# A four-layer network with a scheduled main loop: the TensorE part of the loop traced in program order

## The chip, the cores and the metric

The kernel runs on one core of a Trainium2 chip. The metric is the device time of one execution in microseconds (us). Engines are named as in the profile: PE (TensorE matmul), PEld (its weight loads), DVE (VectorE), ACT (ScalarE), POOL (GpSimd) and SP (SyncE, which issues most DMAs).

## The reference

Input x is fp32, 8 samples of 512 channels and 32 by 32 pixels, that is 512 x 1024 per sample. Four layers follow each other:

```
# layer 0: attention without softmax, scaled by the largest singular value
z = f_x^T g_x ; z2 = (z / sigma_max(z)) h_x ; x = Wv z2 + x
# layer 1: group norm, then full attention over the 1024 pixels
q,k,v = wq h, wk h, wv h ; x = x + wp softmax(q^T k / sqrt(512)) v
# layer 2: non-local block with 128 channels
t,p,g = split(W_w x) ; x = bn(Z_w softmax(t^T p / sqrt(128)) g) + x
# layer 3: binarised 1x1 convolution, batch norm, residual, shifted PReLU
x = prelu(bn(sign(W) scale . sign(x + b)) + x)
```

All 8 samples pass layers 1 to 3 one by one; only the batch norms of layer 0 need all samples at once.

## The kernel before

The kernel is one Python function that records instructions for a scheduling layer. That layer receives the instructions in program order, orders those of each engine by its own estimate of when they can run, and sets all semaphores. Inside `with tc.manual_schedule(engines={PE})` it keeps the recorded order on PE; the other engines are still ordered by it. The kernel already does so for the last part of layer 0 (from L1585), but not for the main loop.

**Main loop.** `for n in range(B): hb, ua = fast(env, n, hb, ua)` (L1661) takes one sample through layers 1 to 3. `fast` (L919) records, in this order: `scores1` (layer 1's score matrix), `make_v`, `values1`, `project2` (layer 2's projections), `scores2`, `values2` and `close2` (layer 2's output), and `leave` (layer 3). PE work of the neighbouring samples is woven in by Python generators: `make_u` of the next sample runs between the steps of layer 2, and the second half of `leave` of the sample before is held in the list `rest3` and run between the first steps of the next sample's `scores1`.

**The seven-product scheme.** The large fp32 matrix products are made as 2 x 2 blocks with seven block products instead of eight (`seven`, L350; the operands' sums are made on DVE in `sums_of` and `differences_of`). A block product is a `term`: two fp32 matmul instructions of 128x512 at L413. Several terms accumulate into one PSUM bank, and partial sums are read out between them, for example

```
term(pa, "S3", "T3", False, False)
plus(va, b2, c22, c22)            # DVE reads the bank (L366)
...
term(pa, "A22", "T4", False, True)
move(c21, va, b2)                 # ACT reads it (L360)
then()                            # in make_u: the sums of ut, L331 to L336
```

The second term may only write the bank when the read before it is done. In `make_u` the last term of the second group is the pair of matmuls shown as `bank<-hs,wu`; the reads of the partial sums are the DVE instructions L366 (`ut<-bank,bu,ut`). In `scores1` the first term is the pair `bank<-ut,h`, its read is the ACT copy L358 (`e<-bank`); the next terms are `us,hs` (S1 T1), `us,hs` (S2 T2, into the first bank), `us,h` (S4 B22) and `ut,h` (S3 T3, into the first bank again, after another L358 copy of it).

**Layer 3.** `leave` (L713) makes sign(x) in fp16 on ACT (L720, `sg`), then for each of two output pairs j four fp16 matmuls (L732, `bank<-sg,sw`), after which come ACT L743, DVE L744, L745, L753 (twice), ACT L775 and L776 (twice each) and DVE L783 (twice), and a DMA to the output. For the last sample the matmuls use `signs`, and L759 (DVE), L762 (ACT), L769 (POOL) take part.

**The boundary between two samples.** There are seven of them. PE's program order there is: the last terms of `make_u` (`h,wu`, `h,wu`, `hs,wu`), then the first score term of the next sample (`ut,h` twice), then four L732 matmuls of the sample before.

**The end.** For the last sample, `inverse_rows` (L887) sums the softmax denominators on PE (L892, from `esum`, which DVE L852 makes) and takes reciprocals on DVE (L893). `count_bad` (L801) checks the denominators' range: a one-column matmul L823, a DVE cast to an integer `bad` (L824), and `values_load` (L825), which every engine runs as a register load (TENSOR_LOAD) of `bad` for the branch `tc.If(verdict[0] > 0)` (L1777). The branch is not taken with these inputs.

Of the kernel before, what the change touches and what calls it, by code (L numbers as in the profile page):

```python
# [17 lines left out]
B = 8  # L18
# [69 lines left out]
def kernel(  # L88
# [39 lines left out]
    def psum_pools(stack, wides, banks):  # L128
        psum.clear()
        for name, n in (("wide", wides), ("bank", banks)):  # L130
            if n:
                psum[name] = stack.enter_context(
                    tc.tile_pool(name=f"{name}{n}", bufs=n, space=PSUM, reuse_waits="tile")
                )
# [342 lines left out]
    def normal(env, xt, alone=False):  # L477

        sc, bi = norm
        ht = env["big"].tile([P, CC, N], F32, tag="h", name="h")  # L480
        for ns in [half(h) for h in range(NH)] if alone else [slice(0, N)]:
            for cc in range(CC):
                s1, b1 = sc[:, cc : cc + 1], bi[:, cc : cc + 1]
                hs, xs = ht[:, cc, ns], xt[:, cc, ns]
                if cc % 2 and not alone:
                    nc.scalar.activation(hs, xs, AF.Identity, bias=b1, scale=s1)
                else:
                    nc.vector.tensor_scalar(hs, xs, s1, b1, ALU.mult, ALU.add)  # L488
        return ht
# [3 lines left out]
    def split_h(env, ht):  # L493
        hs = env["big"].tile([P, 3, 2, HF], F32, tag="hs", name="hs")
        b = [ht[:, chunks[k], half(n)] for k in range(2) for n in range(2)]
        return differences_of(b, [hs[:, i] for i in range(3)])

    def make_u(env, hb, got, early=False):

        ut = env["big"].tile([P, CC, N], F32, tag="uv", name="ut")  # L500
        wa = weights["u"]

        def done():
            us = env["big"].tile([P, 3, 2, HF], F32, tag="us", name="us")
            got.append(
                sums_of(quarters_of(ut, chunks, [half(0), half(1)]), [us[:, i] for i in range(3)])
            )

        def group(i):
            term = product_of(  # L510
                lambda a, b, q, k: wa[a][:, k, bass.ts(i, P)],
                lambda a, b, q, k: hb[b][:, k, :],
            )
            return seven(
                term,
                ut[:, i, half(0)],
                ut[:, i, half(1)],
                ut[:, 2 + i, half(0)],
                ut[:, 2 + i, half(1)],
                bu[:, i : i + 1],  # L520
                bu[:, 2 + i : 3 + i],
                then=done if i else None,
                early=early,
            )

        groups = [group(i) for i in range(2)]
        for _ in range(2 * early):
            for g in groups:
                next(g)
                yield  # L530
        for g in groups:
            yield from g
# [729 lines left out]
    env = {}  # L1262
# [386 lines left out]
    with ExitStack() as main:  # L1649
        psum_pools(main, 0, 8)  # L1650
        big = main.enter_context(tc.tile_pool(name="big", bufs=1, reuse_waits="tile"))
        epool = main.enter_context(tc.tile_pool(name="epool", bufs=EBUFS))
        small = main.enter_context(tc.tile_pool(name="small", bufs=3))
        env.update({"big": big, "e": epool, "small": small})
        got = []
        hb = split_h(env, normal(env, resident[order[0]], True))

        for _ in make_u(env, hb, got, True):
            pass
        ua = got[0]  # L1660
        for n in range(B):  # L1661
            hb, ua = fast(env, n, hb, ua)


    def attention(env, scores, scale, apply):
# [111 lines left out]
    with tc.If(verdict[0] > 0):  # L1777
        with (
# [5 lines left out]
            env = {"big": big, "e": epool, "small": small}  # L1784
# [49 lines left out]
```

## Time and profile before

| | |
|---|---|
| median of 3 runs | 1872.2 us (1871.53 to 1872.94) |
| time of the profiled execution | 1872.37 us |
| its span, first to last instruction | 1870.5 us |
| PE busy, 6196 matmul records | 1850.9 us |
| DVE busy | 1121.5 us |
| ACT busy | 541.7 us |
| granted TensorE clock | 0.998 |

The span is 1.9 us shorter than the execution's time. An fp32 matmul instruction of 128x512 shows as two records that start 0.43 us apart, so it takes 0.86 us of PE's time; the record's own duration (0.59 us) overlaps the next. An fp16 one of the same shape is one record, 0.22 us from the next. Lines are numbered as in the kernel before; in the changed kernel all lines after L1660 are one higher.

### The profile page before, as it was taken

To read this page: it belongs to the slowest core of one execution; us is meant where nothing else is said; L and a number is where in the kernel's file an instruction comes from. 1 tells how busy PE (TensorE), PEld (TensorE's weight loads), DVE (VectorE), ACT (ScalarE), POOL (GpSimd) and SP (SyncE) were. 2 spreads that over 40 slices of the span, in tenths; PEclk is the share of its full clock that TensorE was granted. 3 is DMA by queue.
4 is the path that set the end of the run, shared out by engine and by line. 5 is a ranking of instruction groups with operands and counts; after the bars stand their busy time and mean duration, and the time that the engine had idled before them with its cause. 6 is when DMAs were issued, how large, how long until landed. Compare 5 with 4: busy or idle time off the path is not lost.

```text
span 1870.5 us, 16535 instructions
## 1 busy us (share of the span) xinstructions
PE 1850.9 (99%) x6196; PEld 948.9 (51%) x6196; DVE 1121.5 (60%) x2083; ACT 541.7 (29%) x882; POOL 121.8 (7%) x109
## 2 busy tenths in 40 slices
PE   9999999999999999999999999999999999999997
PEld 4365464544644464544645455544644464544653
DVE  3356777467745767567754676357643766355447
ACT  2042221243213521244202521244203521244114
POOL 1000002000010001100020001100010001000011
PEclk9999999999999999999999999999999999999999
DMA  8620000002000200012000200001000200000001
GB/s 282 201 86 7 1 18 1 1 34 73 12 1 12 90 17 1 0 35 73 12 1 12 90 18 0 1 34 68 12 0 12 90 12 0 1 34 23 12 0 47
DMA packets 32738, 66.52 MB, mean 36 GB/s; under 512 B 4944, under 2 KB 12300, under 8 KB 32524
## 3 DMA queue, kind: packets, MB, share of 16 engines
q1 hardware_dynamic: 31724, 64.96, 10.2%
q8 instruction: 51, 0.84, 0.2%
q10 hardware_dynamic: 864, 0.43, 0.1%
q14 instruction: 35, 0.29, 0.0%
q0 software_dynamic: 64, 0.00, 0.0%
HBM read 46.44 MB, written 18.94 MB: 35 GB/s over the span
## 4 chain that ended last, share of the span: by engine, by line
PE 96%; DVE 2%; ACT 1%; issue 0%; DMA 0%; POOL 0%; ACTq 0%; DVEq 0%
PE bank L413 46%; PE bank L591 21%; PE bank L993 6%; PE bank L840 6%; PE bank L1382 4%; PE bank L692 3%; PE bank L709 3%; PE bank L732 1%; PE bank L437 1%; PE wide L1428 1%; PE bank L1061 1%; PE bank L1486 1%; PE quad L1274 0%; PE bank L863 0%; DVE st L449 0%; DVE xt L446 0%
## 5 line engine op out<-in xcount | busy, mean ns | idle before, releaser
L591 PE MATMUL bank<-e,vt 128*128 128x512 f32 x768 | 336.2, 594 | 0.0
L591 PEld LDWEIGHTS bank<-e,vt 128*128 128x128 f32 x768 | 144.3, 190 | 172.3 <-issue 167.9
L413 PE MATMUL bank<-ut,h 128*128 128x512 f32 x384 | 178.9, 597 | 0.0
L413 PEld LDWEIGHTS bank<-ut,h 128*128 128x128 f32 x384 | 71.3, 190 | 94.7 <-issue 93.0
L413 PE MATMUL bank<-us,hs 128*128 128x512 f32 x256 | 115.6, 593 | 0.0
L840 PE MATMUL bank<-tpg 128*128 128x512 f32 x256 | 115.4, 595 | 0.0
L993 PE MATMUL bank<-e,tpg 128*128 128x512 f32 x256 | 114.7, 595 | 0.0
L364 DVE TENSOR_TENSOR e<-bank,e 128x512 f32<-128x512 f32 x96 | 66.2, 690 | 60.8 <-PE bank L413 47.9
L847 ACT ACTIVATE e<-bank 128x512 f32<-128x512 f32 x128 | 76.3, 597 | 67.0 <-PE bank L840 67.0
L358 ACT COPY e<-bank 128x512 f32<-128x512 f32 x96 | 56.0, 584 | 118.9 <-PE bank L413 118.5
L413 PE MATMUL bank<-wo,h 128*128 128x256 f32 x384 | 89.9, 384 | 0.0
L413 PE MATMUL bank<-h,wu 128*128 128x512 f32 x192 | 89.0, 594 | 0.7 <-DVE h L488 0.7
L993 PEld LDWEIGHTS bank<-e,tpg 128*128 128x128 f32 x256 | 48.1, 190 | 60.4 <-issue 60.0
L244 POOL TENSOR_TENSOR r_r<-r_v,minus_half 128x4 f32<-128x4 f32 (+1 forms) x11 | 10.9, 988 | 1041.5 <-DVE r_v L243 1035.6
L413 PEld LDWEIGHTS bank<-wo,h 128*128 128x128 f32 x384 | 71.4, 190 | 12.6 <-issue 3.8
L413 PEld LDWEIGHTS bank<-us,hs 128*128 128x128 f32 x256 | 48.4, 190 | 57.4 <-issue 54.5
L852 DVE TENSOR_TENSOR esum<-esum,e 128x1024 f32<-128x1024 f32 x48 | 58.8, 1225 | 30.2 <-ACT e L847 29.9
L840 PEld LDWEIGHTS bank<-tpg 128*128 128x128 f32 x256 | 47.7, 190 | 55.0 <-issue 52.4
L720 ACT ACTIVATE sg<-xt,rb 128x512 f16<-128x512 f32 x64 | 44.2, 716 | 107.5 <-DVE xt L711 104.6
L364 DVE TENSOR_TENSOR vt<-bank,vt 128x512 f32<-128x512 f32 x48 | 33.2, 692 | 66.4 <-PE bank L413 65.6
L358 ACT COPY vt<-bank 128x512 f32<-128x512 f32 x64 | 37.3, 583 | 121.4 <-PE bank L413 121.3
L358 ACT COPY ut<-bank 128x512 f32<-128x512 f32 x48 | 28.1, 585 | 127.9 <-PE bank L413 127.9
(361 smaller groups left out, 2917.0 us busy)
## 6 DMA issues: line engine op xcount, KB each, us to landing
xt<-in_x SPq DMA_DIRECT2D x55, 512.0 KB
out<-both SPq DMA_DIRECT2D x63, 256.0 KB
rfull<-r_dram SPq DMA_DIRECT2D x15, 512.0 KB
f_dram<-f SPq DMA_DIRECT2D x8, 256.0 KB
fb<-f_dram SPq DMA_DIRECT2D x8, 256.0 KB
w<-in_w SPq DMA_DIRECT2D x1, 1024.0 KB
blocks_q<-in_w_q SPq DMA_DIRECT2D x16, 64.0 KB
blocks_k<-in_w_k SPq DMA_DIRECT2D x16, 64.0 KB
```

The lines of the kernel that those rows point to most:

```text
L358: nc.scalar.copy(dst, ps)
L364: nc.vector.tensor_tensor(dst, ps, u, ALU.add)
L413: mm(out=ps[:, q * w : (q + 1) * w], lhsT=lt(ka, kb, q, k), rhs=rhs(ka, kb, q, k), start=first and q == 0 and k == 0, stop=last and k == 1 ...
L591: mm(out=ps, lhsT=a[:, t, bass.ts(r_, P)], rhs=e[t], start=first and t == 0, stop=last and t == NTH - 1, skip_group_check=True,)
L692: mm(out=ps[:, i, :], lhsT=xt[:, cc, bass.ts(4 * h + i, P)], rhs=sbw["tpg"][:, cc, 2 * P : 3 * P], start=cc == 0, stop=cc == CC - 1,)
L709: mm(out=ps, lhsT=sbw["z"][:, bass.ts(oc, P)], rhs=att, start=True, stop=True)
L720: nc.scalar.activation(sg[:, cc, :], xt[:, cc, half(h)], AF.Sign, bias=rb3[:, cc : cc + 1])
L840: mm(out=ps, lhsT=pt[:, 0, bass.ts(t, P)], rhs=tt[:, 0, half(h)], start=True, stop=True,)
L847: nc.scalar.activation(e[:, half(h)], ps, AF.Exp, scale=float(P) ** -0.5)
L852: nc.vector.tensor_tensor(esum, esum, e, ALU.add)
L993: mm(out=banks[h], lhsT=gt[:, t, :], rhs=es[t][:, half(h)], start=t == 0, stop=t == NT - 1,)
L1382: mm(out=banks[i][side(h), :], lhsT=w0[i][:, cc, :], rhs=xt[:, cc, half(h)], start=cc == 0, stop=cc == CC - 1,)
```

## The change

The main loop's eight calls of `fast` are recorded inside a manual schedule of PE.

```diff
@@ -1658,8 +1658,9 @@
         for _ in make_u(env, hb, got, True):
             pass
         ua = got[0]
-        for n in range(B):
-            hb, ua = fast(env, n, hb, ua)
+        with tc.manual_schedule(engines={mybir.EngineType.PE}):
+            for n in range(B):
+                hb, ua = fast(env, n, hb, ua)
```

The two built programs, laid side by side, show what this does to the order on each engine. No instruction that computes or moves data is added or removed, and no tile lies at another address. DVE gets one separate wait instruction more at each boundary, for a copy L358 `e` on ACT. SP's and POOL's orders are the same. PE, DVE and ACT differ in the same way at each of the seven sample boundaries, and then at the end of the kernel. At a boundary:

```
PE before: h,wu x4 | ut,h | L732 | hs,wu x2 | ut,h | L732 x3 | us,hs x2 | us,hs x2 | L732 x4 | us,h x2 | ut,h x2
PE after : h,wu x4 | hs,wu x2 | ut,h x2 | L732 x4            | us,hs x2 | us,hs x2 | L732 x4 | us,h x2 | ut,h x2

ACT before: L360, L358, L743, L358, L358 e, L775, L775, L776, L776, L743, L565, L566, ...
ACT after : L360, L358, L743, L358, L775, L775, L776, L776, L358 e, L743, L565, L775, ...

DVE before: ... L753, L753, L783, L364, L783, L744, L364, L745, L364, L753, L753, L568, L783, L611, L783
DVE after : ... L753, L753, L783, L783, L364, L744, L745, L364, L753, L753, L364, L783, L783, L568, L611
```

Here `L358 e` is the copy of the first score bank that the last `ut,h` pair (S3 T3) waits for. DVE's order before the first L753 of this stretch, the two L366 of `make_u` among it, is the same in both programs. The `hs,wu` pair waits for the first of these L366 in both.

At the end of the kernel PE's order has three differences. The two L892 matmul instructions stand in front of the third L993 of their row of eight instead of behind it. The first four L709 stand one L993 earlier. PE's register load L825 stands in front of the last 12 L732 matmuls, right behind L823, where it stood behind them. On DVE one L759 moves in front of one L753, and on ACT one L762 in front of one L775.

## The prediction

> **What bounds the kernel now.** I read the page's totals first, then the chain of waits, then who made PE wait, then the timeline where the two orders differ.
>
> ```profile
> PE 1850.9 (99%) x6196; PEld 948.9 (51%) x6196; DVE 1121.5 (60%) x2083; ACT 541.7 (29%) x882; POOL 121.8 (7%) x109
> ...
> PE 96%; DVE 2%; ACT 1%; issue 0%; DMA 0%; POOL 0%; ACTq 0%; DVEq 0%
> ```
>
> PE is busy for 99% of the span and makes 96% of the chain that ends last. The list of what PE waited for in the whole run begins so, and asked for 240 us to the end it is empty (us in total, times, longest):
>
> ```profile
> PE bank L1382 <- DMA fg<-in_w_fg: 4.3, 1, 4.3
> PE bank L1486 <- ACT ft L1278: 1.1, 1, 1.1
> PE bank L413 <- DVE h L488: 0.7, 1, 0.7
> ```
>
> In the main loop PE has no wait that a better order could remove. It can gain almost nothing there, and each wait that a new order makes is paid in full. So I looked at the first boundary, and at the last part of the kernel.
>
> ```profile
> 411.08 1.02 PE L413 MATMUL bank<-ut,h 128*128 128x512 f32 x2
> 411.31 1.41 DVE L366 SCALAR_TENSOR_TENSOR ut<-bank,bu,ut 128x512 f32<-128x512 f32 x2
> 411.94 0.38 PE L732 MATMUL bank<-sg,sw 128*128 128x512 f16 x1
> 412.15 1.94 PE L413 MATMUL bank<-hs,wu 128*128 128x512 f32 x4
> ...
> 413.93 1.02 PE L413 MATMUL bank<-ut,h 128*128 128x512 f32 x2
> ...
> 414.79 0.81 PE L732 MATMUL bank<-sg,sw 128*128 128x512 f16 x3
> ...
> 415.44 3.60 PE L413 MATMUL bank<-us,hs 128*128 128x512 f32 x8
> ...
> 419.07 0.59 ACT L358 COPY e<-bank 128x512 f32<-128x512 f32 x1 [1.13 <-PE bank L413]
> 419.55 1.33 ACT L775 ACTIVATE up<-both,cb 128x512 f32<-128x512 f32 x2
> ...
> 420.79 1.51 ACT L776 ACTIVATE both<-both,pb,ct 128x512 f32<-128x512 f32 x2
> 421.45 3.60 PE L413 MATMUL bank<-ut,h 128*128 128x512 f32 x8
> ```
>
> The pair hs,wu starts just when the fp16 matmul before it is through. The weight loads tell that it was also only just allowed to:
>
> ```profile
> 412.11 0.30 PEld L413 LDWEIGHTS bank<-hs,wu 128*128 128x128 f32 x2 [0.50 <-DVE ut L366]
> ```
>
> The first L366 runs from 411.31 for 0.75 us (748 ns in that line's own view), so to 412.06. The load starts 0.05 us later and the matmul 0.04 after that. The wait costs nothing now because one fp32 matmul of ut,h (0.86) and one fp16 (0.22) stand in front: 411.08 to 412.15, that is 1.07 us of other work. The other six boundaries show the same 1.07 or 1.08 (623.69 to 624.77, 835.06 to 836.14, 1047.69 to 1048.77, 1256.59 to 1257.66, 1465.40 to 1466.48, 1672.97 to 1674.04).
>
> **What the Trainium skill says.** "TensorE: Matmul & The Clock Gate", Part 2, Step-by-step: weight loads can be pulled ahead, but matmuls stay in program order. The trace agrees: the hs,wu load above is held to 412.11 and PE does not turn to anything behind it. "PSUM — Partial Sum Buffer", Engine vs sequencer instructions: the queues of ScalarE and VectorE are strictly first in, first out; so a copy placed behind four other activations is late by them. The same page, PSUM bank collisions: a bank is to be guarded by semaphores, which is why hs,wu cannot write while L366 reads. "DMA: Bandwidth & Descriptors", Latency and other measured facts, puts a register load at a floor of about 600 ns; here it took 489 ns, and I use that.
>
> **The change part by part.** Sums are made on the profiled execution (1872.37 us), which is 0.2 us above the median.
>
> *Boundary, wait A.* hs,wu now comes first, at 411.08. Its L366 is not earlier: DVE's order up to it is the same, and it stands behind three L711 and two L783 that depend on nothing that moved. So hs,wu still starts at 412.15, PE idles 1.07 us, and ut,h and the fp16 matmul, which filled this time, come afterwards. The fourth fp16 matmul ends at 416.51 instead of 415.44. The time is not won back: PE has no idle time later. 7 x 1.07 = 7.5 us. The L360 read of hs,wu's bank (414.13 to 414.82) is not earlier either, so the sums L331 to L336 gain nothing.
>
> *Boundary, wait B.* The ACT copy L358 of the first score bank, which the ut,h pair at 421.45 must await, was done at 419.66. It is now behind two L775 and two L776, which depend on DVE. Hand-offs are read from the same stretch: PE's last fp32 record start to its ACT reader 0.63 (414.36 to 414.99), fp16 0.42, DVE to ACT or back 0.03, and a queued ACT or DVE instruction starts about 0.1 before the end of the one ahead. With PE 1.07 later: the fourth fp16 record starts 416.30, so L743 runs 416.71 to 417.40. On DVE, L744 then starts at 417.43 instead of 417.29, and with the durations as before the two L753 end at 419.36 and 420.03. ACT: L775 419.40 to 420.12, L775 420.06 to 420.77, L776 420.67 to 421.48, L776 421.38 to 422.18, and the copy 422.08 to 422.67. Weight load and matmul follow 0.05 and 0.04 later, at 422.76, and as after any such wait the first record takes 0.06 more (the 1.94 instead of 1.88 in the hs,wu line). PE was ready at 421.45 + 1.07 = 422.52. So B is 0.24 + 0.06 = 0.30 us. I bound it below by nothing (ACT's chain 0.24 faster) and above by 0.70 (each of the four hand-offs 0.1 worse). 7 x 0.30 = 2.1 us.
>
> *Boundary, further waits.* DVE's L364 come later too. The second pair after S3 T3 (ut,hs) needs the second L364, which my walk ends at 425.4; PE gets there at 426.26. The next S2 T2 needs an ACT copy that ends at about 430.6; PE gets there at 431.4. Both are covered by 0.8 us: cost nothing. The output DMAs start within 0.5 us of before; their buffers are needed several us later: nothing.
>
> *End, L892.* It waits for the last L852, which starts at 1831.27 and takes 1.23.
>
> ```profile
> 1831.27 1.23 DVE L852 TENSOR_TENSOR esum<-esum,e 128x1024 f32<-128x1024 f32 x1 [0.49 <-ACT e L847]
> ...
> 1832.59 0.19 PEld L892 LDWEIGHTS bank<-esum,ones 128*128 128x128 f32 x1 [0.24 <-DVE esum L852]
> 1833.02 1.88 PE L892 MATMUL bank<-esum,ones 128*128 128x512 f32 x4
> ```
>
> One L993 matmul (0.86) stood in front; without it PE arrives at 1832.16, and L892 starts at 1832.50 + 0.09 = 1832.59. PE loses 0.43 + 0.06 = 0.5 us. The reciprocals start 0.36 earlier, so the moved L709 find their input ready.
>
> *End, L825.* The line's own view has the register load on PE's sequencer (count, then duration in ns, then its start):
>
> ```profile
> L825 PEldq TENSOR_LOAD <-bad x1: 489/489/489, 1858.1 to 1858.1; - x1
> ```
>
> and, in the timeline,
>
> ```profile
> 1857.74 2.76 PE L732 MATMUL bank<-sg,signs 128*128 128x512 f16 x12
> 1857.92 0.14 DVE L824 CAST bad<-bank 1x1 int32<-1x1 f32 x1
> ```
>
> The load ran at 1858.1 beside these 12 matmuls. Now they are queued behind it: 1858.1 + 0.49 and a start of 0.06 is 1858.65 instead of 1857.74, 0.9 us. Behind them are the final DVE and ACT chains. DVE's L753 moves from 1859.29 to 1859.72, the others follow; L759 in front of its neighbour takes back nothing. The last L783 (1865.87 before) ends at 1866.22, since one L783 that ran 1.16 us beside a POOL instruction now runs without. So 0.4 us; between 0 and 0.9.
>
> Sum: 7.5 + 2.1 + 0.5 + 0.4 = 10.5 us. 1872.37 + 10.5 = 1882.9 for such an execution, 1882.7 for the median.
>
> **The rivals.** *A alone*: the ACT copy is in time, because my hand-offs are too long. For: B is only 0.24 at the decision. Against: the copy's four predecessors on ACT hang on two DVE ends. 1872.2 + 7.5 + 0.9 = 1880.6. *B grows and spreads*: above 1.1 us per boundary the later covers of 0.8 are used up as well. For: three engines lag at once. 7 x (1.07 + 1.1) + 0.9 = 16.1, 1888.3. *Not slower*: hs,wu does not wait for L366. Then it starts at 411.08, the boundary costs nothing, and the single fp16 matmul no longer interrupts fp32 work (7 x 0.06 = 0.4 less): 1872.2 + 0.9 - 0.4 = 1872.7. For: the releaser is inferred from semaphore events. Against: the load's odd start, 0.05 after L366. It decides if L366's bank is free 1.07 us sooner, at 410.99. That the order does not change is excluded by the two programs.
>
> **How the numbers follow.** Forecast 0.75, A alone 0.10, B larger 0.07, not slower 0.08. About 0.2%, 3.7 us, is what this kernel's measurement tells from no change. Slower is 0.75 + 0.10 + 0.07 = 0.92, the same 0.06, faster 0.02. Range: low is A with nothing from B and half of the end (7.5 + 0.4, 1880.1), taken to 1879.6 for the start of the waits; high is B at 0.7 - 0.3 more per boundary without the rest (+2.8, 1885.5).
>
> **What would show it.** PE waits for DVE ut L366 seven times, about 1.0 us each, and seven times for ACT e L358, about 0.25 us; both are absent now. The first boundary's fourth fp16 matmul ends near 416.5. PE's busy time stays near 1851 while the span grows by 10. It is wrong if hs,wu follows h,wu without a gap, or if PE waits at other places.

## The result, and the profile after

The changed kernel takes 1883.39 us (median of 6 runs, 1882.55 to 1883.68) against 1872.4 us (1871.53 to 1873.11) before: ratio 1.0057, 95% interval 1.0046 to 1.0067. That is 11.0 us slower, where 10.5 were forecast; the profiled execution took 1883.68 us with a span of 1881.8.

The page's totals of the changed kernel, and the first line of its chain of waits:

```profile
span 1881.8 us, 16542 instructions
...
PE 1854.7 (99%) x6196; PEld 948.8 (50%) x6196; DVE 1124.5 (60%) x2083; ACT 540.8 (29%) x882; POOL 121.8 (6%) x109
...
ACT 0%; DVE 0%; issue 0%
```

The same 6196 matmul records are spread over 11.3 us more. The chain is of no use here: followed back from the end it stops at 1875.14 us, after six pieces, and never reaches TensorE, so what held TensorE has to be read elsewhere. What PE waited for (us in total, times, longest):

```profile
PE bank L413 <- DVE ut L366: 6.1, 7, 0.9
...
PE bank L732 <- DVE bad L824: 0.8, 1, 0.8
...
PE bank L892 <- DVE esum L852: 0.2, 1, 0.2
```

These three were absent before. The seven waits of the first line are the seven boundaries between images. The first boundary in the timeline:

```profile
412.08 1.40 DVE L366 SCALAR_TENSOR_TENSOR ut<-bank,bu,ut 128x512 f32<-128x512 f32 x2
412.87 0.30 PEld L413 LDWEIGHTS bank<-hs,wu 128*128 128x128 f32 x2 [1.69 <-DVE ut L366]
412.87 1.98 PE L413 MATMUL bank<-hs,wu 128*128 128x512 f32 x4 [0.87 <-DVE ut L366]
...
414.69 1.88 PE L413 MATMUL bank<-ut,h 128*128 128x512 f32 x4
...
416.41 1.03 PE L732 MATMUL bank<-sg,sw 128*128 128x512 f16 x4
...
417.27 3.60 PE L413 MATMUL bank<-us,hs 128*128 128x512 f32 x8
...
420.17 1.38 ACT L775 ACTIVATE up<-both,cb 128x512 f32<-128x512 f32 x2 [0.39 <-DVE both L753]
...
421.46 1.51 ACT L776 ACTIVATE both<-both,pb,ct 128x512 f32<-128x512 f32 x2
...
422.87 0.56 ACT L358 COPY e<-bank 128x512 f32<-128x512 f32 x1
...
423.48 0.30 PEld L413 LDWEIGHTS bank<-ut,h 128*128 128x128 f32 x2 [0.86 <-ACT e L358]
```

hs,wu starts 0.05 us after the first of the two L366 ends (412.08 + 0.74), with nothing in front of it to fill the time; 10.6 us later the S3 T3 pair waits for the copy L358 behind two L775 and two L776. The list shows 0.87 us for the first wait and does not name the second. The reason is that it counts from the modelled end of the matmul before, 0.59 us after its start, while a fully fed TensorE starts a fp32 record every 0.43. From start to start, less the 0.43, the first wait is 1.03 us and the second 0.19; the 0.16 us between the two ways of counting hide most of the second one.

The end of the kernel:

```profile
1841.66 1.23 DVE L852 TENSOR_TENSOR esum<-esum,e 128x1024 f32<-128x1024 f32 x1 [0.49 <-ACT e L847]
...
1842.94 1.98 PE L892 MATMUL bank<-esum,ones 128*128 128x512 f32 x4 [0.23 <-DVE esum L852]
...
1868.81 0.14 DVE L824 CAST bad<-bank 1x1 int32<-1x1 f32 x1
...
1869.50 2.75 PE L732 MATMUL bank<-sg,signs 128*128 128x512 f16 x12 [0.81 <-DVE bad L824]
...
1869.82 2.79 POOL L769 TENSOR_TENSOR both<-both,up 128x512 f32<-128x512 f32 x2 [2.76 <-ACT both L762]
...
1871.42 1.47 DVE L759 TENSOR_SCALAR up<-both,nc,ps 128x512 f32<-128x512 f32 x1
```

and the register load on TensorE's sequencer in its line's own view:

```profile
L825 PEldq TENSOR_LOAD <-bad x1: 492/492/492, 1869.0 to 1869.0; - x1
```

The 12 fp16 matmuls stand behind this load: they start 0.97 us after L823's matmul, against 0.09 before.

What follows on VectorE and ScalarE was, in the kernel before:

```profile
1860.61 1.40 DVE L759 TENSOR_SCALAR up<-both,nc,ps 128x512 f32<-128x512 f32 x1
1860.79 0.72 ACT L775 ACTIVATE up<-both,cb 128x512 f32<-128x512 f32 x1 [0.48 <-DVE both L753]
1862.05 0.81 ACT L762 ACTIVATE both<-both,qb,ct 128x512 f32<-128x512 f32 x1 [0.54 <-DVE up L759]
1862.77 0.80 ACT L776 ACTIVATE both<-both,pb,ct 128x512 f32<-128x512 f32 x1
```

and is in the changed one, behind the L759 at 1871.42 shown above:

```profile
1872.92 0.81 ACT L762 ACTIVATE both<-both,qb,ct 128x512 f32<-128x512 f32 x1 [1.74 <-DVE up L759]
1873.65 0.72 ACT L775 ACTIVATE up<-both,cb 128x512 f32<-128x512 f32 x1
1874.40 0.81 ACT L776 ACTIVATE both<-both,pb,ct 128x512 f32<-128x512 f32 x1
```

Counted from L823, L759 ends at the same time in both (4.36 and 4.35 us), and so does L762 (5.21 and 5.20). But L775, which was done ahead of L762, now comes behind it.

To set the parts against each other I cut the span at two matmuls, the first of L709 (the first image's second half) and that of L823:

| part | before | after | difference |
|---|---|---|---|
| span start to first L709 | 390.39 | 391.16 | 0.77 |
| first L709 to L823 | 1467.26 | 1477.38 | 10.12 |
| L823 to span end | 12.85 | 13.28 | 0.43 |

The first part has nothing of the change in it: it lies between 390.0 and 391.9 in the twelve kernels profiled here, in no order that follows their edits. The second and third make 10.55 us.

### The profile page after: what moved, and what is told of

Read it like the earlier page. It is cut to its first block, busy times and chain, and to the rows that moved or that the text cites. A ratio compares the mean times of both kernels' runs of the same rounds, so it can differ in the third digit from the quotient of the medians.

```text
span 1881.8 us, 16542 instructions
## 1 busy us (share of the span) xinstructions
PE 1854.7 (99%) x6196; PEld 948.8 (50%) x6196; DVE 1124.5 (60%) x2083; ACT 540.8 (29%) x882; POOL 121.8 (6%) x109
## 5 line engine op out<-in xcount | busy, mean ns | idle before, releaser
L993 PE MATMUL bank<-e,tpg 128*128 128x512 f32 x256 | 114.7, 595 | 0.0
L358 ACT COPY e<-bank 128x512 f32<-128x512 f32 x96 | 56.0, 583 | 123.4 <-PE bank L413 123.4
L993 PEld LDWEIGHTS bank<-e,tpg 128*128 128x128 f32 x256 | 48.1, 190 | 60.4 <-issue 60.0
L852 DVE TENSOR_TENSOR esum<-esum,e 128x1024 f32<-128x1024 f32 x48 | 58.8, 1226 | 30.1 <-ACT e L847 29.9
L358 ACT COPY vt<-bank 128x512 f32<-128x512 f32 x64 | 37.4, 584 | 121.3 <-PE bank L413 121.2
L358 ACT COPY ut<-bank 128x512 f32<-128x512 f32 x48 | 28.1, 586 | 127.9 <-PE bank L413 127.9
```

The lines of the kernel that those rows point to most:

```text
L358: nc.scalar.copy(dst, ps)
L852: nc.vector.tensor_tensor(esum, esum, e, ALU.add)
L993: mm(out=banks[h], lhsT=gt[:, t, :], rhs=es[t][:, half(h)], start=t == 0, stop=t == NT - 1,)
```

## The experiments

Theory: two waits at each boundary, A (hs,wu for VectorE's L366, 7 x 1.07) and B (S3 T3 for ScalarE's copy, 7 x 0.30), and 0.9 us at the end. The cover of a matmul is the work that stands in front of it on TensorE while the instruction that it waits for is being finished. The rivals in the expectations are that TensorE's order costs in itself, or that other waits come up. All edits are made to the changed kernel unless said otherwise, and none leaves work out. Added lines shift the later numbers by a few; where a line shown is affected, the text says so. "Stretch" is the middle part of the table above, less the 1467.26 us of before. The experiments ran on several chips; each is compared with the kernel before on its own chip.

**1. ScalarE's copy back ahead of L776.** The layer-3 step is split where ScalarE's L775 begins, and the second half is recorded after the copy. TensorE's order is exactly that of the changed kernel.

```diff
@@ leave
                     sums = y1, y2
+                    if stop and j == 0:
+                        yield
@@ fast, in the loop over scores1
             if rest3 and k % 2 == 0:
+                if k == 2:
+                    next(rest3[0])
```

> TensorE's order is that of the changed kernel, instruction for instruction; only ScalarE's copy L358 of the first score bank stands ahead of the two L776 again (still behind the two L775), and one VectorE addition of the scores is one place later. Theory (two exposed waits, A by VectorE's L366, B by ScalarE's copy): B goes (7 x 0.30 = 2.1 us), A stays at 7 x 1.07; about 1881.3 us, 2.1 below the changed kernel, and the wait for L366 unchanged. Rival (all of the loss is TensorE's order, ScalarE's place of the copy costs nothing): 1883.4, no change. Rival (the copy was not the last to be waited for): the gap before S3 T3 stays at about 0.2 us with another releaser.

Measured: 1881.44 us, before 1873.12 on that chip (ratio 1.0046, 1.0033 to 1.006). Stretch +7.99 against +10.12. From its timeline (L777 and L778 are L775 and L776):

```profile
419.88 1.39 ACT L777 ACTIVATE up<-both,cb 128x512 f32<-128x512 f32 x2 [0.39 <-DVE both L755]
...
421.17 0.56 ACT L358 COPY e<-bank 128x512 f32<-128x512 f32 x1
421.28 1.88 PE L413 MATMUL bank<-us,h 128*128 128x512 f32 x4
421.63 1.52 ACT L778 ACTIVATE both<-both,pb,ct 128x512 f32<-128x512 f32 x2
...
423.00 1.45 PE L413 MATMUL bank<-ut,h 128*128 128x512 f32 x3
```

The copy ends at 421.73, and the S3 T3 pair follows us,h after 1.72 us, four records of 0.43, without a gap. B is worth 10.12 - 7.99 = 2.13 us and is set by the place of the copy in ScalarE's queue. The wait for L366 is the same 6.1 us as in the changed kernel.

**2. Half the cover for hs,wu.** The last step of `make_u` is not taken at the end of the image but inside the first score product of the next, between its two matmuls. (`ua` is filled in when that step is taken; only its A11, which exists earlier, is used before.)

```diff
@@ fast, at the end of an image
             fill(2)
-            for _ in steps:
-                pass
+            owed.append(steps)
@@ scores1
+            def lt(a, b, q, k):
+                if k and owed:
+                    for _ in owed.pop():
+                        pass
+                return hb[b][:, k, bass.ts(i, P)]
```

> The last product of the next image's u (hs,wu) is put between the two matmuls of the first score product, so one fp32 matmul (0.86 us) stands in front of it instead of none; ScalarE's copy is ahead of the layer-3 activations again. Theory: of wait A 1.07 - 0.86 = 0.21 us is left, with the longer first record about 0.3, B is gone: 7 x 0.3 + 0.9 for the end = 3.0 us above before, about 1875.4. Rival (hs,wu doesn't wait for VectorE's L366 but costs by its place or by the number of changes of weights): no dependence on 0.86 us of cover, 1881 to 1883. Rival (the wait is of the same length wherever hs,wu stands, since L366 itself comes later with it): A stays at 1.07, 1881.

Measured: 1875.16 us, 2.0 above before (ratio 1.0013, 1.0006 to 1.0019). Stretch +1.98. Timeline:

```profile
410.95 1.02 PE L413 MATMUL bank<-ut,h 128*128 128x512 f32 x2
411.19 1.40 DVE L366 SCALAR_TENSOR_TENSOR ut<-bank,bu,ut 128x512 f32<-128x512 f32 x2
411.98 0.30 PEld L413 LDWEIGHTS bank<-hs,wu 128*128 128x128 f32 x2 [0.83 <-DVE ut L366]
```

hs,wu still starts when the first L366 has ended, but only 0.17 us after TensorE was ready for it (410.95 + 0.86). The wait shrank from 1.03 by the 0.86 us of one fp32 matmul: it has the size that the cover leaves. ScalarE's copy came ahead of L775 by itself, so B is absent.

**3. The whole cover.** The same deferral, taken after the whole first score product:

```diff
@@ fast, in the loop over scores1
+            if owed:
+                for _ in owed.pop():
+                    pass
             if rest3 and k % 2 == 0:
```

> hs,wu is put behind the whole first score product, 1.72 us of cover; ScalarE's copy stands behind one L775 only. Theory: A (needs 1.07) and B are both gone, only the 0.9 us of the end remain: about 1873.3, and no wait of TensorE in the seven boundaries. Rival (the time is not won back, something else is late by the same): 1880 or more. Rival (A alone is cured, B stays): 1875.4.

Measured: 1880.61 us, 7.5 above before (ratio 1.0038, 1.0025 to 1.0052). A miss by 7 us: the first rival's figure. Stretch +6.58. Its timeline says why:

```profile
412.54 1.02 PE L413 MATMUL bank<-ut,h 128*128 128x512 f32 x2
...
412.77 1.40 DVE L366 SCALAR_TENSOR_TENSOR ut<-bank,bu,ut 128x512 f32<-128x512 f32 x2
...
414.23 0.30 PEld L413 LDWEIGHTS bank<-ut,h 128*128 128x128 f32 x2 [1.50 <-DVE ut L366]
414.23 1.12 PE L413 MATMUL bank<-ut,h 128*128 128x512 f32 x2 [0.67 <-DVE ut L366]
```

Now the second matmul of the score product waits, and for the second L366. In the code that is the `plus(vb, b1, c11, c11)` of `second()` in the group i = 1: it finishes the part of A11 that the second half of the product reads. So two matmuls hang on two L366 that end 0.66 us apart: hs,wu on the first (by its bank), the second half of ut,h on the second (by its data). I had looked only at the first. With ut,h put in front, its second half arrives 0.83 us too early; in the changed kernel hs,wu stands before it and covers it. hs,wu itself no longer waits, and B is gone too, since the copy got ahead of one L775 and both L776.

**4. hs,wu behind the fp16 matmuls.** The deferred step is taken after the four fp16 matmuls instead (the lines added in 3 move below the `rest3` block).

> hs,wu is put behind the first score product and the four fp16 matmuls, 2.58 us of cover; ScalarE keeps the order of the changed kernel there, with the copy behind two L775 and two L776. Theory: A is gone, and since the fp16 products that feed L775 and L776 now run 1.72 us earlier against S3 T3, the copy is in time by 1.4 us although its place is the bad one: B gone, about 1873.3. Rival (B comes from the place in ScalarE's queue alone): 7 x 0.30 stay, 1875.4. Rival (the later hs,wu makes the sums that S4 needs late): a new wait of the us product, above 1874.

Measured: 1882.41 us, 9.3 above before (ratio 1.0049, 1.0036 to 1.0063). Stretch +8.33. The wait of ut,h's second half is that of run 3. My expectation for B failed as well, as its timeline shows (L756, L778 and L779 are L753, L775 and L776):

```profile
417.71 0.69 ACT L360 ACTIVATE ut<-bank,bu 128x512 f32<-128x512 f32 x1 [1.03 <-PE bank L413]
...
418.44 1.22 DVE L336 TENSOR_TENSOR us<-ut,us 128x1024 f32<-128x1024 f32 x1
...
419.58 1.41 DVE L756 SCALAR_TENSOR_TENSOR both<-both,sa,xt 128x512 f32<-128x512 f32 x2
420.36 1.38 ACT L778 ACTIVATE up<-both,cb 128x512 f32<-128x512 f32 x2 [0.34 <-DVE both L756]
...
423.06 0.56 ACT L358 COPY e<-bank 128x512 f32<-128x512 f32 x1
```

A later hs,wu makes L360 later; VectorE's L336, which needs it, stands in front of the two L756 and holds them, these hold ScalarE's activations, and the copy behind them ends at 423.62 when TensorE was ready at 423.53. I had moved the fp16 products earlier and overlooked that VectorE's queue carries the sums of hs,wu as well. That this queueing is the cause is read off the trace; it was not tried by an edit.

**5. The first L366 ahead of L711.** The S3 T3 step of `make_u` is recorded before the products of L709. This moves its two h,wu matmuls on TensorE as well as the L366 that reads them.

```diff
@@ fast, at the end of an image
+            fill(1)
             close2(xt, att, 1)
             rest3.append(leave(env, xt, dst, [1], stop=True))
             next(rest3[0])
-            fill(2)
+            fill(1)
```

> Program order for TensorE as in the changed kernel, but the S3 T3 product of the next image's u (h,wu) is recorded ahead of the two products of L709. VectorE so has the L366 that hs,wu waits for ahead of the four L711 instead of behind them; the second L366 stays behind them. Theory (A is the wait for this L366, late since it queues behind L711; the runs before have shown that the second half of the first score product waits for the second L366): hs,wu starts without a gap, ut,h's second half has hs,wu (1.72 us) in front and is covered too, ScalarE's copies are in time: only the end remains, before + 0.9 us, or + 0.5 since no fp16 matmul interrupts the fp32 ones. Rival (an order of TensorE as recorded costs by itself, wherever VectorE's L366 stands): after, before + 10 or more. Rival (the products of L709, now 1.72 us later, make the fp16 matmuls late): a new wait there, before + 2 to + 8.

Measured: 1873.69 us against 1872.91 (ratio 1.0004, 0.9996 to 1.0012), not to be told from before by the times. Stretch +0.07. Timeline:

```profile
405.70 3.60 PE L709 MATMUL bank<-att,z 128*128 128x512 f32 x8
...
406.71 1.41 DVE L366 SCALAR_TENSOR_TENSOR ut<-bank,bu,ut 128x512 f32<-128x512 f32 x2
...
409.35 2.48 DVE L711 TENSOR_TENSOR xt<-bank,xt 128x512 f32<-128x512 f32 x4
...
410.86 1.88 PE L413 MATMUL bank<-hs,wu 128*128 128x512 f32 x4
411.74 0.75 DVE L366 SCALAR_TENSOR_TENSOR ut<-bank,bu,ut 128x512 f32<-128x512 f32 x1
```

TensorE keeps the recorded order, with hs,wu ahead of ut,h as in the changed kernel, and yet hs,wu has nothing to wait for: its L366, the second of the first pair shown, was done 2.7 us before. The last L366 ends at 412.49, and ut,h's second half, whose turn comes at 413.43, is covered by hs,wu and its own first half. ScalarE's copy came ahead of both L775 by itself, so B is absent too. So program order as such costs nothing at the boundaries; the loss was the place of L366 in VectorE's queue against what TensorE has in front. That it was the queue, and not the h,wu product that L366 reads, the trace of the changed kernel tells: the last record of that product starts at 409.70, 2.4 us ahead of L366, and VectorE works without a gap from 407.70 to L366, with three L711 from 410.28 to 412.16 as the last in front.

**6, 7, 8. The end.** Run 6 sets the end of the changed kernel back; run 7 is the kernel before with program order from the last image's second half on (the context is entered ahead of `unpacked`); run 8 is 5 and 6 together. The edit of 6:

```diff
@@ count_bad
         nc.vector.tensor_copy(bad, ps[0:1, 0:1])
+        yield
         verdict.append(nc.values_load(bad, min_val=0, max_val=P))
@@ fast, last image
+            values2(0, range(2, 3))
             r = inverse_rows(env, esum, B + n)
-            att = values2(0, range(2, NT))
+            att = values2(0, range(3, NT))
...
             for _ in after:
                 pass
+            next(count)
```

> The changed kernel with its end alone set back: one more L993 matmul recorded ahead of L892, and the register load of L825 recorded behind the last products. The seven boundaries are as in the changed kernel. Theory (L892 0.5, L825 0.4 at the end, 0.9 on TensorE): 0.9 us below the changed kernel, about before + 10; TensorE's gap ahead of the last 12 fp16 matmuls gone, its gap at L892 from 0.82 to about 0.43. Rival (ScalarE's and VectorE's chain behind the last matmuls sets the end and takes the gain back): 0.5 below only. Rival (the load, now last, stands in the chain to the branch on every engine): not faster, or up to 0.5 us slower than the changed kernel.

> The kernel before (scheduler's order for TensorE) with program order only from the last image's second half on, so the boundaries are as before and the end as in the changed kernel. Theory: before + 0.9 us. Rival (the end carries more than its 0.9, the boundaries less): before + 2 or more. Rival (the end costs nothing): before + 0.

> Both: L366 early (as in the run with that change alone) and the end set back. Theory: all that program order costs is taken away by hand, the time is that of before, or 0.4 us less since the fp16 matmuls no longer interrupt fp32 ones: before - 0.4 to before + 0.3, not to be told from before. Rival (the scheduler's order gains something in places that have not been looked at): before + 1 or more.

Measured, against 1872.91 before: run 6 1883.4 us (ratio 1.0055, 1.0042 to 1.0069), run 7 1874.08 (1.0006, 0.9998 to 1.0015), run 8 1873.07 (1.0003, 0.9994 to 1.0011). Run 7 is 1.2 us above before by its median, which its interval does not tell from none; its trace shows 0.49 in the stretch and 0.41 behind L823. Run 6 gained nothing like 0.9. L892 no longer waits, but one matmul fewer lies between it and L709, and in the timeline of run 6 L709 has to wait for att:

```profile
1851.32 0.63 DVE L1003 TENSOR_TENSOR att<-bank,rfull 128x512 f32<-128x512 f32 x1
...
1852.00 2.41 PE L709 MATMUL bank<-att,z 128*128 128x512 f32 x5 [0.34 <-DVE att L1003]
```

From start to start that is 0.50 us of idle, and with the longer first record 0.61, for the 0.50 saved at L892: two waits on one chain (L852, the reciprocals, att), of which one goes only if there is work for the other too.

**9. The exact end.** Run 8 with one more matmul of the second half ahead of L709, which gives TensorE its old order at the end.

```diff
-            values2(1, range(0, 2))
+            values2(1, range(0, 3))
             close2(xt, att, 0)
-            values2(1, range(2, 6))
+            values2(1, range(3, 6))
```

> As the run with L366 early and the end set back, but with one more of the second half's L993 matmuls ahead of L709, so that TensorE has the order of the kernel before at its end, instruction for instruction. Theory: the new wait of L709 for att (0.61 us in that run) goes, and against before there remain 7 x 0.06 us less for the fp16 matmul that no longer interrupts fp32 ones and some 0.17 more in the last chain of VectorE: before - 0.25 us, not to be told from before by the time, but the span's matmul gaps show it. Rival (program order has a cost that has not been found): before + 0.5 or more.

Measured: 1872.5 us against 1873.15 (ratio 0.9997, 0.9989 to 1.0006). Stretch -0.45, L823 to the end +0.01. The waits of PE in the whole run begin as those of the kernel before:

```profile
PE bank L1386 <- DMA fg<-in_w_fg: 4.3, 1, 4.3
PE bank L1490 <- ACT ft L1282: 1.1, 1, 1.1
PE bank L413 <- DVE h L488: 0.7, 1, 0.7
```

All of the loss is undone with TensorE's main loop still in program order. The trace has it 0.44 us ahead of before; the times cannot tell the two apart.

**10. The register load alone.** Of the edit of 6 only the part that records the load later.

> The changed kernel with only the register load of L825 recorded behind the last products. Read off the two runs in which it was set back together with L892: the stretch from L823's matmul to the end of the last L783 is 8.98 us in the changed kernel and 8.39 there. Theory: 0.6 us below the changed kernel, about before + 10.4, with no wait for att at L709, since L892 keeps its place. Rival (the end takes back all of it): no difference in this stretch. Rival (the wait of L709 for att came from the load): it appears here too.

Measured: 1883.22 us (ratio 1.0053, 1.004 to 1.0067). The fp16 matmuls follow L823 after 0.09 us; the stretch from L823 to the end of the last L783 is 8.40 us (changed kernel 8.98, before 8.22), to the end of the span 12.90 (13.28 and 12.85). L709 has no wait for att at the end (the one in this run's list, 0.2 us, is in the first image, at 391.18). By the trace the load costs 0.38 us at the end. In this run VectorE and ScalarE have a third order there, so the 0.38 us belong to the load and the orders that come with it. The median, 0.2 below the changed kernel, does not resolve it.

All runs, in us above before; the third column is worked out from the start-to-start gaps of the boundaries (0.10 more for the first record after a wait, 0.06 less where no fp16 matmul interrupts) and at L892 or L709:

| kernel | stretch, measured | stretch, from the gaps | behind L823 | by the medians |
|---|---|---|---|---|
| changed | 10.12 | 7 x (1.07 + 0.30) + 0.50 = 10.1 | 0.43 | 11.0 |
| 1 | 7.99 | 7 x 1.07 + 0.50 = 8.0 | 0.44 | 8.3 |
| 2 | 1.98 | 7 x (0.17 + 0.10 - 0.06) + 0.50 = 2.0 | 0.45 | 2.0 |
| 3 | 6.58 | 7 x (0.83 + 0.10 - 0.06) + 0.50 = 6.6 | 0.45 | 7.5 |
| 4 | 8.33 | 7 x (0.87 as in 3 + 0.14 + 0.10) + 0.50 = 8.3 | 0.42 | 9.3 |
| 5 | 0.07 | -7 x 0.06 + 0.50 = 0.1 | 0.43 | 0.8 |
| 6 | 10.18 | 7 x 1.37 + 0.61 = 10.2 | 0.13 | 10.5 |
| 7 | 0.49 | 0.50 | 0.41 | 1.2 |
| 8 | 0.13 | -7 x 0.06 + 0.61 = 0.2 | 0.20 | 0.2 |
| 9 | -0.45 | -7 x 0.06 = -0.4 | 0.01 | -0.7 |
| 10 | 10.10 | 10.1 | 0.05 | 10.1 |

## Why the prediction held, step by step

- *Wait A, 7 x 1.07.* Right. Start to start 1.03 us of idle TensorE at each boundary and 0.10 for the longer first record, less 0.06 for the fp16 matmul that no longer cuts in: 1.07. Run 2 shows that the wait shrinks by what is put in front, run 5 that it goes when L366, with the product it reads, goes ahead in VectorE's queue.
- *Wait B, 7 x 0.30.* Right in place and in its sum: 0.19 + 0.10 = 0.30 (unrounded), and run 1 takes off 2.13 us for 2.1. Its two terms were forecast as 0.24 and 0.06. In waits A and B and at L892 alike the matmul started 0.05 us after the end it waited for, not 0.09, and its first record was 0.10 longer, not 0.06; that these two errors cancel is luck. The walk put the copy at 422.08 and the S3 T3 matmul at 422.76 on the clock of before; the trace has 422.87 and 423.48, less the 0.77 us by which this execution began late 422.10 and 422.71.
- *Further waits: nothing.* Right: no other gap in the stretch, which closes within 0.1 us. But the prediction missed a neighbour, the second half of ut,h on the second L366. In the changed kernel it is covered, so the sum was not hurt; it sank my expectations for runs 3 and 4.
- *L892, 0.5.* Right: 0.40 idle and 0.10. That the moved L709 finds att ready holds only because L892 moved with it (run 6).
- *L825, 0.9 on TensorE and 0.4 at the end.* The 0.9 is right; the 0.4 is right by luck, since two errors on its path cancel. TensorE's delay is 0.97 - 0.09 = 0.88 us. The last L783 was to end 0.35 us later; counted from L823 it ended 0.76 later. I had counted as a gain that one L783, slow in the kernel before (1.16 us), is so no longer (0.75). But those 0.41 us were not on the path: before, it ended 7.10 us after L823, and the next L783 had to wait for an L776 until 7.21. What is late is ScalarE: the L753 that L775 reads now stands behind the slow L759, and L775 (0.72 us) behind L762, so the last L776 ends at 8.46 instead of 7.70, and the last L783 0.52 behind it as before. This is read off the traces and was not tried by an edit of these orders alone. Behind the last L783, 0.33 us came back (4.63 to 4.30 us to the end of the span), which I had not foreseen, so the span behind L823 is 0.43 longer. In that part VectorE's own register load took 548 ns instead of 854; whether this is the cause was not tried.
- *TensorE's busy time stays near 1851.* Wrong: 1854.7. Each of the 14 waits shows the full modelled tail of the record before (0.59 instead of the 0.43 that the next start leaves visible) and a first record 0.10 longer: 14 x (0.163 + 0.105) = 3.75 of the 3.8 us. By the same count the list had to miss wait B, which I had expected there; it shows on the weight load alone.

Of the rivals, A alone and B larger fall by the gaps, and "not slower" by run 2: hs,wu starts with the end of L366 at two different covers.

## What to carry to other kernels

When TensorE is busy for 99%, an order that looks arbitrary can be the one that puts just enough work in front of each late operand: before fixing an order by hand, list for every moved matmul which reader or writer it waits for, and when that one is done in its own engine's queue. Do this for each matmul of a group by itself, since halves of one product can hang on different instructions. A wait can be cured at its source: recording earlier the product whose VectorE read came late cost nothing here (stretch +0.07), where moving the waiting matmul left 2.0 to 8.3 us and, in runs 3 and 4, exposed another wait.

## What the runs showed of the hardware

- The first fp32 record that starts after a wait occupies 0.53 us to the next start instead of 0.43, at A, B and L892 alike; so even a wait of 0.17 us cost 0.27. It is not a mark of a wait alone: in the kernel before, the first ut,h record behind L307's matmuls, which have half as many rows (at 434.62), takes 0.53 too, and the list names no wait there. At all these places the weight load starts together with the matmul, not a record ahead of it; whether this is the cause was not tried.
- A register load in TensorE's queue (492 ns) holds the matmuls behind it, 0.88 us in all with its wait for VectorE; recorded behind them it cost TensorE nothing. "TensorE: Matmul & The Clock Gate" in the Trainium skill, Part 2, Step-by-step, says that matmuls stay in program order; the runs agree, and the load stands in the same order.
- VectorE's L759 takes 0.55 us, but each one that began while GpSimd's L769 was running ended 0.28 to 0.29 us after that L769, in all twelve traces (under its own line number in each): it took 0.98 to 1.00 us, or 1.40 to 1.47, by how much of the L769 was left. One that began 0.1 us ahead of an L769 kept its 0.55, and this L769 took 1.56 to 1.58 us instead of about 1.27. No run varied this by an edit.
